# Attention and involution in one fp32 kernel: row sums by block transposes, another order of the first loads, and compute engines that keep the program's order

## The chip, the core and the metric

One core of a Trainium2 chip runs the whole program. Times are device microseconds of that core, in one launch. The engines are named as in the profile: PE is TensorE (PEld is its weight loads), DVE is VectorE, ACT is ScalarE, POOL is GpSimd, SP is SyncE, whose queue issues most of the DMAs.

## What is computed

The input `x` is 4 images of 512 channels and 64 x 64 pixels in fp32. Two layers follow each other. Cut to what matters:

```python
# layer 0: attention over the 4096 pixels of an image, 128 inner channels
q, k, v = wq @ x + bq, wk @ x + bk, wv @ x + bv        # each 128 x 4096
attn = softmax(q.T @ k, axis=-1)                       # 4096 x 4096
x = x + wo @ (v @ attn.T) + bo
# layer 1: involution, 7 x 7 taps whose weights are computed from the pixel
o = relu(s1 * (W1 @ x) + b1)                           # 128 channels
w = Ws @ relu(sr * (Wr @ o) + br) + bs                 # 49 taps x 8 groups, per pixel
x = x + s3 * (W3 @ sum_over_taps(w[tap, group] * shifted(o, tap))) + b3
```

## The kernel before

All that runs is `fast_path`. It computes the softmax without subtracting a maximum, and at its end it looks at every reciprocal of a row sum. If one lies outside of a safe range, the flag `verdict` sends the program into `general_path`, which repeats everything in the careful way. With these inputs the branch isn't taken.

**Keys and values.** For each image `b`, `keys_values` goes over 8 chunks of 512 pixels. A chunk costs four matmuls for `pk` and four for `pv` (512 input channels are 4 x 128), then `turn` transposes the values (`pvt`). Every fp32 matmul shows in the trace as two records.

**Attention.** Then `attention` goes over 8 blocks of 512 queries (the last two blocks of the last image are split into halves of 256) and for each block over 32 steps `j`. A step is one `score` matmul (`pss`, two steps ahead), an exponential on ACT (`pt`), one matmul of values by weights (`po`), and on DVE one addition `pacc<-pacc,pt` that sums the weights (lines 566 to 572).

**What is done between the steps.** After each step, and after every two matmuls of `keys_values`, `chores()` (line 223) takes one step of three generators. `finishing` holds `finish_block` of the block before: the row sums are added over the partitions by a matmul with a matrix of ones (`pl`, line 447), DVE takes the reciprocals in four pieces (`rl`, line 454), multiplies (`on`, line 457), then come `pwo` with an addition on DVE (line 463), `p1`, the transposes `pp` and the red layer `pr`; its `pause` calls and bare `yield`s are the numbers of steps between these. `closing` holds `turn_unit` and `close_chunk`: transposes `pa` of a finished sum, the matmuls `py` with W3 and an addition on DVE (line 367) for each. `pace()` takes taps of `involution`: each tap is a product on DVE (`prod`, line 291) and an addition on POOL (`acc`, line 315). A unit of the involution is 4 image rows; an image has 16 units.

**The planner.** `until`, `takes` and `free` keep an account of when PE, DVE and POOL will be free, with fixed costs (lines 64 to 68). It decides where in the program a tap is written: not while DVE has more than 3.5 us or POOL more than 7.5 us of work ahead of PE (line 269).

**The tail.** After the last step of the last image, `tail` is set (line 589), the waiting loops end at once, and a plain loop takes one step of `finishing`, one of `closing` and one tap in turn. In the tail every second tap is added not by POOL but by PE, as matmuls with the identity into `accp` (line 301):

```python
    while finishing or closing or units or more:
        step(finishing, 1)
        step(closing, 1)
        more = step(taps, 1)
```

**Buffers.** `pk` and `pss` share two PSUM buffers, `pl`, `pwo`, `p1`, `pp`, `pr`, `pq`, `pa` and `py` two others (tag `mm`); `pw` has one. The products have four buffers (`prods`), the exponentials five.

**The order on each engine.** The program gives a list of instructions. The library's scheduler may reorder them on each engine: it keeps the dependences and picks what its own model of the machine says is ready. What it picked is what the trace shows, and it isn't always the order in which the lines of the program are reached.

Of the kernel before, what the change touches and what calls it, by code (L numbers as in the profile page):

```python
# [8 lines left out]
F32 = mybir.dt.float32  # L9
AF = mybir.ActivationFunctionType  # L10
ALU = mybir.AluOpType
AX = mybir.AxisListType

B, C, H, W = 4, 512, 64, 64
N = H * W
P = 128
CT = C // P
CH = 512
NCH = N // CH
# [13 lines left out]
O_WK, O_WV, O_WQ, O_WO, O_W1, O_W3 = (i * 512 for i in range(6))  # L33
O_WP = 6 * 512
O_WT = O_WP + P
O_WR = O_WT + NTAP * G
# [7 lines left out]
V_BVC = V_BV + P  # L44
# [20 lines left out]
DVE_OP, POOL_OP = 0.7, 1.28  # L65
DVE_TAPS, POOL_TAPS = (0.16, 0.27), (0.19, 0.55)
ROW_US, X_US, PIX_US, LAND_US = 2.2, 3.8, 1.5, 3.0
HOP_US = 0.8

SAFE = (1e-30, 1e20)  # L70

# [2 lines left out]
def fast_path(  # L74
# [20 lines left out]
    nc = tc.nc  # L95

    def pool(name, bufs, **kw):
        return ctx.enter_context(tc.tile_pool(name=name, bufs=bufs, **kw))

    const = pool("const", 1)  # L100
    xpool = pool("x", 6)
# [3 lines left out]
    work1 = pool("work1", 1)  # L105
    work2 = pool("work2", 2)
    prods = pool("prods", 4)
    scratch = pool("scratch", 1, space=bass.MemoryType.DRAM)
    ps = pool("ps", 2, space=bass.MemoryType.PSUM)
    ps1 = pool("ps1", 1, space=bass.MemoryType.PSUM)  # L110

    wt = const.tile([P, O_WR], F32, name="wt")
    vec = const.tile([P, NVEC], F32, name="vec")
    ones = const.tile([P, P], F32, name="ones")
    ident = const.tile([P, P], F32, name="ident")
    rls = const.tile([B * NCH, CH], F32, name="rls")
    zero = const.tile([WP, PAD, P], F32, name="zero")
    ring = const.tile([P, RING, K, P], F32, name="ring")
    pix = [
# [3 lines left out]
    x_r = x.rearrange("b (t p) n -> b p t n", p=P)  # L123
# [16 lines left out]
    def until(us):  # L140
        while pe < us and not tail:
            yield "wait"

    def pe_us(us):
        nonlocal pe
        pe += us

    def takes(engine, us):
        free[engine] = max(free[engine], pe) + us
        return free[engine]  # L150

    def load_x(kind, b, c):
        xt = xpool.tile([P, CT, CH], F32, tag="x", name=f"{kind}_{b}_{c}")
        takes("dma", X_US)
        nc.sync.dma_start(xt, x_r[b, :, :, c * CH : (c + 1) * CH])
        return xt

    nc.sync.dma_start(wt[:, :O_WQ], wts[:, :O_WQ])
    nc.scalar.dma_start(vec, vecs)
    xa = {(0, c): load_x("xa", 0, c) for c in range(2)}  # L160
    xb = {}
    nc.scalar.dma_start(wt[:, O_WQ:], wts[:, O_WQ:O_WR])
    nc.gpsimd.memset(ones, 1.0)
    make_identity(nc, ident)
    nc.gpsimd.memset(zero, 0.0)

    def w_slice(off, t):
        return wt[:, off + t * P : off + (t + 1) * P]

    def v1(i):  # L170
        return vec[:, i : i + 1]

    def mm(o, lhsT, rhs, start=True, stop=True, shared=1):
        pe_us(rhs.free_size() * PE_COLUMN / shared)
        nc.tensor.matmul(o, lhsT=lhsT, rhs=rhs, start=start, stop=stop)  # L175

    def step(queue, n):
        while n and queue:
# [250 lines left out]
    def finish_block(b, c, off, n, po, sums):  # L429

        late = b == B - 1 and c >= NCH - 2
        name = f"{b}_{c}_{off}"
        xt = xb[b, c][:, :, off : off + n]

        def pause(us, steps):
            if late:
                yield from until(us + HOP_US)
            else:
                for _ in range(steps):
                    yield  # L440

        on = work2.tile([P, CH], F32, tag="on", name=f"on_{name}")[:, :n]
        nc.scalar.copy(on, po)
        yield from pause(free["dve"], 3)
        pl = ps.tile([P, CH], F32, tag="mm", name=f"pl_{name}")[:, :n]
        for i in range(CH // n):
            mm(pl, ones, sums[:, i * n : (i + 1) * n], i == 0, i == CH // n - 1)
        rl = work1.tile([P, CH], F32, tag="rl", name=f"rl_{name}")[:, :n]
        for i in range(n // P):
            if i == 0 or not late:  # L450
                yield
            cols = slice(i * P, (i + 1) * P)
            takes("dve", 0.9)
            nc.vector.reciprocal(rl[:, cols], pl[:, cols])  # L454
        row = b * NCH + c
        nc.sync.dma_start(rls[row : row + 1, off : off + n], rl[:1, :])
        nc.vector.tensor_tensor(on, on, rl, ALU.mult)
        yield from pause(takes("dve", DVE_OP * n / CH), 5)
        for t in range(CT):
            pw = ps.tile([P, CH], F32, tag="mm", name=f"pwo_{name}_{t}")[:, :n]  # L460
            mm(pw, w_slice(O_WO, t), on)
            takes("dve", DVE_OP * n / CH)
            nc.vector.scalar_tensor_tensor(  # L463
                xt[:, t, :], pw, bo[:, t : t + 1], xt[:, t, :], ALU.add, ALU.add
            )
            for _ in range(t % 2 if late else 1 + (t != 1)):
                yield
        p1 = ps.tile([P, CH], F32, tag="mm", name=f"p1_{name}")[:, :n]
        for t in range(CT):
            mm(p1, w_slice(O_W1, t), xt[:, t, :], t == 0, t == CT - 1)  # L470
            if t == 1 and not late:
                yield
        o1 = work1.tile([P, CH], F32, tag="o1", name=f"o1_{name}")[:, :n]
        nc.scalar.activation(o1, p1, AF.Relu, bias=v1(V_B1), scale=v1(V_S1))

        def last_bias():

            for t in range(CT):
                nc.scalar.activation(xt[:, t, :], xt[:, t, :], AF.Identity, bias=v1(V_B3 + t))  # L479
                if t % 2:  # L480
                    yield

        if late:
            yield from until(pe + HOP_US)
        else:
            yield from last_bias()

        tiles = n // P
        pp = ps.tile([P, CH // P, P], F32, tag="mm", name=f"pp_{name}")[:, :tiles]
        for t in range(tiles):  # L490
            nc.tensor.transpose(pp[:, t, :], o1[:, t * P : (t + 1) * P], ident)  # L491
        pe_us(0.5)
        o1t = work1.tile([P, CH // P, P], F32, tag="o1t", name=f"o1t_{name}")[:, :tiles]
        nc.scalar.copy(o1t, pp)
        top = c * RW + off // W
        for h in range(2):
            row = PAD + top + h
            nc.sync.dma_start(
                pix[b % 2][row : row + 2 * tiles - 1 : 2, PAD : PAD + W, :]
                .rearrange("r w c -> w r c"),  # L500
                o1t[h * W : (h + 1) * W],
            )
        us = takes("dma", PIX_US) + LAND_US
        pr = ps.tile([P, CH], F32, tag="mm", name=f"pr_{name}")[:, :n]
        mm(pr, w_slice(O_WP, 0), o1)
        red = redpool.tile([P, CH], F32, tag="red", name=f"red_{name}")[:, :n]
        nc.scalar.activation(red, pr, AF.Relu, bias=v1(V_BP), scale=v1(V_SP))
        for i in range(tiles // NT):
            reds[b, top // UR + i] = red, i * NT * P

        rows = top + n // W
        written[b] = rows, us
        units.extend((b, u) for u in range(top // UR, rows // UR))
        pump()
        yield
        if late:
            yield from last_bias()
# [61 lines left out]
    for b in range(B):  # L579
        kv = keys_values(b)  # L580
        if b == 0:

            pb = ps.tile([P, CT], F32, tag="mm", name="pb")
            for t in range(CT):
                mm(pb[:, t : t + 1], w_slice(O_WO, t), v1(V_BVC))
            bo = const.tile([P, CT], F32, name="bo")
            nc.vector.tensor_tensor(bo, pb, vec[:, V_BO : V_BO + CT], ALU.add)
        attention(b, *kv)
# [5 lines left out]
        more = step(taps, 1)  # L594


    ok = const.tile([B * NCH, CH], F32, name="ok")
    nc.vector.tensor_scalar(ok, rls, SAFE[0], None, ALU.is_ge)
    nc.vector.scalar_tensor_tensor(ok, rls, SAFE[1], ok, ALU.is_le, ALU.mult)
    okr = const.tile([B * NCH, 1], F32, name="okr")  # L600
    nc.vector.tensor_reduce(okr, ok, AX.X, ALU.min)
    pn = ps.tile([1, 1], F32, tag="mm", name="pn")
    nc.tensor.matmul(pn, lhsT=okr, rhs=ones[: B * NCH, :1], start=True, stop=True)
    nc.vector.tensor_scalar(verdict, pn, float(B * NCH) - 0.5, None, ALU.is_lt)


@with_exitstack
# [300 lines left out]


def attention_then_involution(tc, x, wts, vecs, out):  # L910
    nc = tc.nc
    with tc.tile_pool(name="verdict", bufs=1) as vpool:
        verdict = vpool.tile([1, 1], mybir.dt.int32, name="verdict")
        fast_path(tc, x, wts, vecs, out, verdict)
        again = nc.values_load(verdict[0:1, 0:1], min_val=0, max_val=1)
        with tc.If(again > 0):
            general_path(tc, x, wts, vecs, out)
# [85 lines left out]
```

## Time and profile before

| | |
|---|---|
| time, median of 3 runs | 2691.6 us (2691.48 to 2693.56) |
| span of the profiled run | 2689.5 us |
| PE busy | 2653.6 us, 99% |
| DVE busy | 1910.1 us, 71% |
| POOL busy | 1818.1 us, 68% |
| ACT busy | 894.4 us, 33% |
| DMA, mean rate over the span | 89 GB/s |
| first matmul of a key chunk starts at | 11.09 us |
| attention of the last block ends, DVE writes its last `sums` at | 2593.66 us |
| `verdict` written at | 2682.73 us |

In a group of the profile, the text names line, engine, operation, tile written `<-` tiles read and shapes; after the bar come the busy time in us and the mean ns of one, and after the second bar the idle time of that engine just before, with what ended it. In the timeline the columns are start, duration, engine, line, operation, tiles, and in brackets how long the engine sat idle before and for whom. Records of matmuls overlap in the timeline, so what one costs is read from the distance between starts: a 512-column fp32 matmul takes 0.86 us (two records).

### The profile page before, as it was taken

How to read it: one execution, taken by the hardware profiler on the slowest of the kernel's cores; microseconds unless marked ns; L12 is line 12 of the kernel's file. 1: busy time of each engine (PE TensorE's matmuls, PEld its weight loads, DVE VectorE, ACT ScalarE, POOL GpSimd, SP SyncE). 2: the span in 40 equal slices, each digit the busy share in tenths (PEclk: the TensorE clock that was granted, in tenths of full speed). 3: DMA queues.
4: the chain of work that ended last, by engine and by line, in shares of the span. 5: the costliest groups of instructions: out<-in, count | busy, mean ns of one | idle time of the engine just before them, and what ended most of it. 6: DMA issues, size and time to landing. Idle time of an engine off the chain costs nothing.

```text
span 2689.5 us, 23125 instructions
## 1 busy us (share of the span) xinstructions
PE 2653.6 (99%) x6932; PEld 1237.2 (46%) x6932; DVE 1910.1 (71%) x2635; ACT 894.4 (33%) x1495; POOL 1818.1 (68%) x1187
## 2 busy tenths in 40 slices
PE   8999999999999999999999999999999999999998
PEld 4444444444444444444444444444444444446874
DVE  0347888887475787888656678778847577888787
ACT  1333333332333333333233333333323333333420
POOL 0006788788681787878875478778877367887875
PEclk9999999999999999999999999999999999999999
DMA  7023223235614233323450423333453242332532
GB/s 239 21 56 68 68 74 78 59 90 137 182 39 104 59 90 90 91 70 77 131 148 23 104 59 90 90 91 90 106 148 103 44 99 67 79 71 59 116 79 83
DMA packets 109285, 240.07 MB, mean 89 GB/s; under 512 B 6296, under 2 KB 24928, under 8 KB 109024
## 3 DMA queue, kind: packets, MB, share of 16 engines
q1 hardware_dynamic: 108864, 237.10, 35.7%
q8 instruction: 56, 0.92, 0.1%
q10 hardware_dynamic: 288, 1.42, 0.1%
q14 instruction: 77, 0.63, 0.1%
HBM read 195.66 MB, written 42.77 MB: 89 GB/s over the span
## 4 chain that ended last, share of the span: by engine, by line
PE 96%; POOL 2%; DVE 1%; issue 0%; DMA 0%; ACT 0%; SPq 0%; POOLq 0%; ACTq 0%; DVEq 0%
PE pss L175 33%; PE po L175 33%; PE pq L175 4%; PE p L175 4%; PE pwo L175 4%; PE pv L175 4%; PE py L175 4%; PE pk L175 3%; PE pw L175 2%; POOL acc L315 2%; PE pl L175 1%; PE pr L175 1%; DVE prod L291 1%; PE accp L175 1%; PE pp L491 1%; PE pvt L383 1%
## 5 line engine op out<-in xcount | busy, mean ns | idle before, releaser
L315 POOL TENSOR_TENSOR acc<-acc,prod 128x768 f32<-128x768 f32 (+3 forms) x1059 | 1693.6, 1617 | 847.9 <-DVE prod L291 802.3
L175 PE MATMUL pss<-q,k 128*128 128x512 f32 (+1 forms) x2176 | 1051.1, 570 | 2.5 <-ACT q L425 2.5
L175 PE MATMUL po<-pt,v 128*128 128x512 f32 (+1 forms) x2176 | 1047.5, 568 | 0.0
L538 ACT ACTIVATE pt<-pss 128x512 f32<-128x512 f32 x1024 | 611.1, 597 | 1220.4 <-PE pss L175 1180.5
L291 DVE TENSOR_TENSOR prod<-ring,pw 128x512 f32<-128x512 f32 (+3 forms) x1092 | 894.2, 848 | 125.5 <-DMA ring<-pix 74.8
L569 DVE TENSOR_TENSOR pacc<-pacc,pt 128x512 f32<-128x512 f32 x956 | 662.1, 693 | 396.0 <-ACT pt L538 392.8
L175 PEld LDWEIGHTS po<-pt,v 128*128 128x128 f32 x2176 | 410.8, 190 | 469.7 <-issue 446.1
L175 PEld LDWEIGHTS pss<-q,k 128*128 128x128 f32 x2176 | 404.9, 190 | 460.8 <-issue 441.5
L175 PE MATMUL pwo<-on,wt 128*128 128x512 f32 (+1 forms) x272 | 132.7, 574 | 10.8 <-DVE xb L463 7.9
L367 DVE SCALAR_TENSOR_TENSOR xb<-py,vec,xb 128x512 f32<-128x512 f32 (+1 forms) x132 | 96.5, 731 | 58.2 <-PE py L175 55.7
L175 PE MATMUL py<-accT,wt 128*128 128x512 f32 (+1 forms) x264 | 131.1, 581 | 1.1 <-ACT accT L352 1.0
L454 DVE RECIPROCAL rl<-pl 128x128 f32<-128x128 f32 x128 | 120.2, 945 | 14.3 <-PE pl L175 14.3
L324 POOL TENSOR_TENSOR acc<-acc 128x512 f32<-128x512 f32 x120 | 123.4, 1028 | 9.4
L479 ACT ACTIVATE xb<-xb,vec 128x512 f32<-128x512 f32 (+1 forms) x136 | 93.8, 694 | 83.1 <-PE p L175 79.0
L175 PE MATMUL p<-xb,wt 128*128 128x512 f32 (+1 forms) x272 | 120.3, 567 | 0.0
L175 PE MATMUL pv<-xa,wt 128*128 128x512 f32 x256 | 118.9, 602 | 0.0
L175 PE MATMUL pk<-xa,wt 128*128 128x512 f32 x256 | 118.4, 600 | 0.3 <-DMA xa<-x_dram 0.3
L175 PE MATMUL pq<-xb,wt 128*128 128x512 f32 (+1 forms) x272 | 116.1, 567 | 0.0
L463 DVE SCALAR_TENSOR_TENSOR xb<-pwo,bo,xb 128x512 f32<-128x512 f32 (+1 forms) x136 | 96.9, 716 | 22.9 <-PE pwo L175 22.5
L291 DVE TENSOR_TENSOR acc<-ring,pw 128x1024 f32<-128x1024 f32 (+1 forms) x84 | 78.9, 958 | 29.0 <-PE pw L175 28.7
L567 DVE COPY pacc<-pt 128x512 f32<-128x512 f32 x34 | 23.5, 692 | 88.1 <-ACT pt L538 88.0
L175 PEld LDWEIGHTS pwo<-on,wt 128*128 128x128 f32 x272 | 51.9, 192 | 70.0 <-issue 48.6
(53 smaller groups left out, 891.5 us busy)
## 6 DMA issues: line engine op xcount, KB each, us to landing
ring<-pix SPq DMA_DIRECT2D x30, 1344.0 KB, 13.8
ring<-pix SPq DMA_DIRECT2D x38, 896.0 KB, 11.9
xa<-x_dram SPq DMA_DIRECT2D x32, 1024.0 KB, 5.9
xb<-x_dram SPq DMA_DIRECT2D x32, 1024.0 KB, 5.8
out_dram<-xb SPq DMA_DIRECT2D x31, 1024.0 KB, 4.2
ring<-pix SPq DMA_DIRECT2D x66, 448.0 KB, 9.9
ring<-pix SPq DMA_DIRECT2D x8, 2240.0 KB, 14.7
pix<-o1t SPq DMA_DIRECT2D x60, 128.0 KB, 2.5
```

The lines of the kernel that those rows point to most:

```text
L175: nc.tensor.matmul(o, lhsT=lhsT, rhs=rhs, start=start, stop=stop)
L291: nc.vector.tensor_tensor(prod[:, :, p0 : p0 + n, :].rearrange("p t d (g c) -> p t d g c", g=G), image.rearrange("p t d (g c) -> p t d g c ...
L315: nc.gpsimd.tensor_tensor(acc[:, :, d0 : d0 + n, :], acc[:, :, d0 : d0 + n, :], prod[:, :, :n, :], ALU.add,)
L324: nc.gpsimd.tensor_tensor(acc[:, :, :n, :], acc[:, :, :n, :], acc[:, :, n : 2 * n, :], ALU.add)
L367: nc.vector.scalar_tensor_tensor(xt[:, t, :], py, v1(V_S3 + t), xt[:, t, :], ALU.mult, ALU.add)
L383: nc.tensor.transpose(pvt[:, j, :], vs[:, j * P : (j + 1) * P], ident)
L454: nc.vector.reciprocal(rl[:, cols], pl[:, cols])
L463: nc.vector.scalar_tensor_tensor(xt[:, t, :], pw, bo[:, t : t + 1], xt[:, t, :], ALU.add, ALU.add)
L479: nc.scalar.activation(xt[:, t, :], xt[:, t, :], AF.Identity, bias=v1(V_B3 + t))
L491: nc.tensor.transpose(pp[:, t, :], o1[:, t * P : (t + 1) * P], ident)
L538: nc.scalar.activation(pt, pss, AF.Exp)
L569: nc.vector.tensor_tensor(paccs[k], paccs[k], pt, ALU.add)
```

## The change

It has three parts.

The **row sums** are added in another way. DVE adds the sums in groups of 32 columns with a transposed read (`blocks`, 128 x 16 instead of 128 x 512), a matmul with `quads` (four identities of 32 in each direction) of 16 columns adds over the partitions, one reciprocal takes 16 columns, a block transpose spreads them over 512 columns again (`spread`), and the multiplication follows. The reciprocals stay in SBUF, so a small DMA for each block (line 456) goes. The four steps between the reciprocals go too.

The **first loads** come in the order of their use: the weights of the keys, the first chunk of `x` in four pieces, the weights of the values, the second chunk, then the rest of the weights, all on one queue. The matmul `pb` for a bias is tied to its place in the program.

The **order**: `manual_schedule` makes PE, DVE, ACT and POOL take their instructions exactly as the program lists them. It is meant to let the planner's order stand as written.

```diff
-    nc.sync.dma_start(wt[:, :O_WQ], wts[:, :O_WQ])
+
     nc.scalar.dma_start(vec, vecs)
-    xa = {(0, c): load_x("xa", 0, c) for c in range(2)}
-    xb = {}
-    nc.scalar.dma_start(wt[:, O_WQ:], wts[:, O_WQ:O_WR])
+    nc.sync.dma_start(wt[:, :O_WV], wts[:, :O_WV])
+    xa, xb = {(0, 0): xpool.tile([P, CT, CH], F32, tag="x", name="xa_0_0")}, {}
+    for t in range(CT):
+        nc.sync.dma_start(xa[0, 0][:, t, :], x_r[0, :, t, :CH])
+    nc.sync.dma_start(wt[:, O_WV:O_WQ], wts[:, O_WV:O_WQ])
+    xa[0, 1] = load_x("xa", 0, 1)
+    nc.sync.dma_start(wt[:, O_WQ:], wts[:, O_WQ:O_WR])
...
+        blocks = work2.tile([P, CH // TB], F32, tag="blocks", name=f"blocks_{name}")
+        takes("dve", DVE_OP)
+        nc.vector.tensor_reduce(
+            blocks, sums.rearrange("p (k q) -> p k q", q=TB), AX.X, ALU.add, apply_transpose=True
+        )
         yield from pause(free["dve"], 3)
-        pl = ps.tile([P, CH], F32, tag="mm", name=f"pl_{name}")[:, :n]
+        pl = ps.tile([P, CH // TB], F32, tag="mm", name=f"pl_{name}")[:, : n // TB]
         for i in range(CH // n):
-            mm(pl, ones, sums[:, i * n : (i + 1) * n], i == 0, i == CH // n - 1)
-        rl = work1.tile([P, CH], F32, tag="rl", name=f"rl_{name}")[:, :n]
-        for i in range(n // P):
-            if i == 0 or not late:
-                yield
-            cols = slice(i * P, (i + 1) * P)
-            takes("dve", 0.9)
-            nc.vector.reciprocal(rl[:, cols], pl[:, cols])
-        row = b * NCH + c
-        nc.sync.dma_start(rls[row : row + 1, off : off + n], rl[:1, :])
-        nc.vector.tensor_tensor(on, on, rl, ALU.mult)
+            mm(pl, quads, blocks[:, i * n // TB : (i + 1) * n // TB], i == 0, i == CH // n - 1)
+        row = (b * N + c * CH + off) // TB
+        rl = rls[:, row : row + n // TB]
+        nc.vector.reciprocal(rl, pl)
+        spread = work1.tile([P, CH], F32, tag="rl", name=f"spread_{name}")[:, :n]
+        nc.vector.transpose(
+            spread.rearrange("p (k q) -> p k q", q=TB),
+            rl.unsqueeze(2).broadcast_to([P, n // TB, TB]),
+        )
+        nc.vector.tensor_tensor(on, on, spread, ALU.mult)
+        takes("dve", 0.3 + DVE_OP * n / CH)
         yield from pause(takes("dve", DVE_OP * n / CH), 5)
...
-                mm(pb[:, t : t + 1], w_slice(O_WO, t), v1(V_BVC))
+                tc.keep_in_program_order(mm(pb[:, t : t + 1], w_slice(O_WO, t), v1(V_BVC)))
...
-    ok = const.tile([B * NCH, CH], F32, name="ok")
+    ok = const.tile([P, B * N // TB], F32, name="ok")
...
-    nc.tensor.matmul(pn, lhsT=okr, rhs=ones[: B * NCH, :1], start=True, stop=True)
-    nc.vector.tensor_scalar(verdict, pn, float(B * NCH) - 0.5, None, ALU.is_lt)
+    nc.tensor.matmul(pn, lhsT=okr, rhs=ones[:, :1], start=True, stop=True)
+    nc.vector.tensor_scalar(verdict, pn, P - 0.5, None, ALU.is_lt)
...
-        fast_path(tc, x, wts, vecs, out, verdict)
+        with tc.manual_schedule(engines={E.PE, E.DVE, E.Activation, E.Pool}):
+            fast_path(tc, x, wts, vecs, out, verdict)
```

More of the change, by code (lines that the diff above doesn't have):

```diff
@@ L68 @@
 HOP_US = 0.8
+TB = 32
 SAFE = (1e-30, 1e20)
@@ L115, in fast_path @@
     ident = const.tile([P, P], F32, name="ident")
-    rls = const.tile([B * NCH, CH], F32, name="rls")
+    rls = const.tile([P, B * N // TB], F32, name="rls")
+    quads = const.tile([P, P], F32, name="quads")
     zero = const.tile([WP, PAD, P], F32, name="zero")
@@ L165, in fast_path @@
     nc.gpsimd.memset(zero, 0.0)
+    for i in range(P // TB):
+        corner = ident[:, i * TB : (i + 1) * TB]
+        if i == 0:
+            nc.gpsimd.tensor_copy(quads[:, :TB], corner)
+        else:
+            nc.gpsimd.tensor_tensor(quads[:, :TB], quads[:, :TB], corner, ALU.add)
+    for i in range(1, P // TB):
+        nc.gpsimd.tensor_copy(quads[:, i * TB : (i + 1) * TB], quads[:, :TB])
     def w_slice(off, t):
@@ L174, in mm @@
         pe_us(rhs.free_size() * PE_COLUMN / shared)
-        nc.tensor.matmul(o, lhsT=lhsT, rhs=rhs, start=start, stop=stop)
+        return nc.tensor.matmul(o, lhsT=lhsT, rhs=rhs, start=start, stop=stop)
     def step(queue, n):
@@ L594, in fast_path @@
         more = step(taps, 1)
-    ok = const.tile([B * NCH, CH], F32, name="ok")
+    ok = const.tile([P, B * N // TB], F32, name="ok")
     nc.vector.tensor_scalar(ok, rls, SAFE[0], None, ALU.is_ge)
     nc.vector.scalar_tensor_tensor(ok, rls, SAFE[1], ok, ALU.is_le, ALU.mult)
-    okr = const.tile([B * NCH, 1], F32, name="okr")
+    okr = const.tile([P, 1], F32, name="okr")
     nc.vector.tensor_reduce(okr, ok, AX.X, ALU.min)
     pn = ps.tile([1, 1], F32, tag="mm", name="pn")
-    nc.tensor.matmul(pn, lhsT=okr, rhs=ones[: B * NCH, :1], start=True, stop=True)
-    nc.vector.tensor_scalar(verdict, pn, float(B * NCH) - 0.5, None, ALU.is_lt)
+    nc.tensor.matmul(pn, lhsT=okr, rhs=ones[:, :1], start=True, stop=True)
+    nc.vector.tensor_scalar(verdict, pn, P - 0.5, None, ALU.is_lt)
 @with_exitstack
@@ L910, in attention_then_involution @@
 def attention_then_involution(tc, x, wts, vecs, out):
-    nc = tc.nc
+    nc, E = tc.nc, mybir.EngineType
     with tc.tile_pool(name="verdict", bufs=1) as vpool:
         verdict = vpool.tile([1, 1], mybir.dt.int32, name="verdict")
-        fast_path(tc, x, wts, vecs, out, verdict)
+        with tc.manual_schedule(engines={E.PE, E.DVE, E.Activation, E.Pool}):
+            fast_path(tc, x, wts, vecs, out, verdict)
         again = nc.values_load(verdict[0:1, 0:1], min_val=0, max_val=1)
```

## The prediction

> **What bounds the kernel now.** I read the page's parts 1, 2 and 4 first, then busy time by stage, then the timeline of PE and DVE where PE has gaps.
>
> ```profile
> PE 2653.6 (99%) x6932; PEld 1237.2 (46%) x6932; DVE 1910.1 (71%) x2635; ACT 894.4 (33%) x1495; POOL 1818.1 (68%) x1187
> PE 96%; POOL 2%; DVE 1%; issue 0%; DMA 0%; ACT 0%; SPq 0%; POOLq 0%; ACTq 0%; DVEq 0%
> ```
>
> PE is 99% busy and holds 96% of the chain that ended last: what leaves PE leaves the time, what makes PE wait is added. The stages (stretch, its length, then busy us of PE, PEld, DVE, ACT, POOL):
>
> ```profile
> 2080.00:2500.00 420.00, 419.99 (x1126) 203.77 (x1124) 315.56 (x439) 150.88 (x250) 289.94 (x188) 1.00 0.30 70
> 2594.00:2683.00 89.00, 79.32 (x286) 43.15 (x284) 73.00 (x98) 7.77 (x17) 59.73 (x38) 0.98 0.35 86
> ```
>
> Until the attention ends (2594 us) PE doesn't wait and DVE has a quarter of its time free. In the tail, 89 us, DVE works 73 and PE 79: both nearly full, and each feeds the other. The gaps, in order:
>
> ```profile
> 8.97 1.84 PE L175 MATMUL pb<-vec,wt 128*128 128x1 f32 x8 [8.97 <-DMA wt<-wts_dram]
> 11.09 5.19 PE L175 MATMUL pk<-xa,wt 128*128 128x512 f32 x8 [0.28 <-DMA xa<-x_dram]
> ...
> 1315.66 0.95 DVE L291 TENSOR_TENSOR prod<-ring,pw 128x768 f32<-128x768 f32 x1 [1.47 <-POOL acc L315]
> 1316.53 0.75 DVE L463 SCALAR_TENSOR_TENSOR xb<-pwo,bo,xb 128x512 f32<-128x512 f32 x1
> 1317.33 1.41 PE L175 MATMUL pwo<-on,wt 128*128 128x512 f32 x2 [2.62 <-DVE xb L463]
> ```
>
> PE starts at 11.09 us, `pb` (which the program lists after all keys) ahead of everything. At 1314 the addition of line 463, for a `pwo` that was done at about 1312, stands on DVE behind a tap that waits for POOL, and PE waits for its PSUM buffer. The same gap is at 664 and 1966.
>
> In the tail the order matters most:
>
> ```profile
> 2613.08 1.02 PE L175 MATMUL py<-accT,wt 128*128 128x512 f32 x2
> 2613.94 1.45 PE L175 MATMUL accp<-prod,ident 128*128 128x512 f32 x4
> 2615.23 1.88 PE L175 MATMUL py<-accT,wt 128*128 128x512 f32 x4
> ...
> 2614.81 1.81 DVE L291 TENSOR_TENSOR prod<-ring,pw 128x768 f32<-128x768 f32 x2
> 2616.54 0.74 DVE L367 SCALAR_TENSOR_TENSOR xb<-py,vec,xb 128x512 f32<-128x512 f32 x1
> 2617.20 0.94 DVE L291 TENSOR_TENSOR prod<-ring,pw 128x768 f32<-128x768 f32 x1
> ```
>
> Two `py` run back to back, which the program never lists, and DVE has taps to do while PE works: line 367 starts without an idle bracket.
>
> [...] here the first `pk` records are 0.98, 0.85, 0.85 us apart, then 0.43. Prices: [...] (the trace has 128-column transposes, each with its load, 0.11 us apart[...]; the trace has 690 for `sums`).
>
> **Part by part: what it gives.**
>
> Row sums. 30 matmuls `pl` of 512 columns (0.86 us from start to start) and 8 of 256 (0.43) are 29.2 us of PE. A 16-column matmul costs [...] 0.21 us (from below 0.05, if both loads hide, like the two records of `pn`, 0.026 apart; from above 0.43, the 0.214 between records of the one-column `pb`, which ran at the slow clock). 38 x 0.21 = 8.2, so **-21.0 us** (-13 to -27). On DVE four reciprocals of 945 ns (3.78) become a reduction and a transpose of 512 columns (0.69 each, by the price)[...]. That, the DMA of line 456 and a microsecond of POOL for `quads` count nothing: DVE waited 392.8 us for `pt` already, SP and POOL have gaps there. `pl` now waits for the reduction, 0.69 us later; in most blocks it came 6.98 us after `sums` started.
>
> First loads. Needed are 256 KB weights and 256 KB of `x`, with 99 KB of `vec` beside them. In the DMA view 226 KB are moved by 3.0 us, 443 by 3.75 and 792 by 4.5, so the 625 come by 4.2; a landing takes up to about 1 us more. First `pk` at 5.3 instead of 11.09: **-5.8** (-4.5 to -6.9). Later pieces arrive every 0.7 us, faster than cold matmuls use them. `pb` moves to after the keys: **+1.0**.
>
> Boundaries. In the program line 463 comes right after its `pwo`, ahead of later taps, and taps are listed only while the account has POOL at most 7.5 us behind. The three gaps (2.8 us each beyond a record) and the slow records after two of them (2.6) go: **-11** (-6 to -13).
>
> Shorter finish. The four steps between reciprocals (4 x 1.72 us) go, so image rows reach the involution earlier. Near the end taps are paced at 1.56 lines a us and POOL has only gaps of 3 to 5 us to give: the tail begins some 5 us of taps further on, **-3**.
>
> **What it costs.** On PE, DVE order in the middle hardly matters: the listed additions come earlier than now, and PE is already in program order there, but for three things.
>
> - At the end of the keys the transposes of the last chunk come before `pq`. Now one `pq` (0.86) fills the wait for ACT's copy (0.2 + 0.58); in program order PE waits. 4 x 0.87 = **+3.5**.
> - The first `pw` of each image is listed right behind `pr`, and needs ACT to have read `pr`. Now a `pss` runs first. In program order ACT still has two biases (0.69 each), an exponential (0.60), `o1t` (0.56) and the red layer (0.75) ahead: `pw` waits about 1.5. 4 times: **+6**.
> - `accp`, `pa`, `py` in the tail, below.
>
> The tail. There each round lists a step of `closing`, then a tap; a closing takes 9 rounds, so the taps in front of a `py` are fixed: an odd one, which PE adds. The listed sequence is tap (odd), its `accp`, `py`, line 367, tap (even), tap (odd), and so on. DVE now stands at line 367 until PE has done `accp` and `py`, and PE has nothing until DVE's next odd tap. With 0.86 us for each 512 columns, 0.1 and 0.2 for the two hand-overs: `accp` of three lines 1.29, of two 0.86, of four 1.72; `py` 0.86 (half size 0.43). DVE idles 2.45 us for each of three `py` of chunk 5 and 2.9 for the fourth, 2.0, 2.0, 2.0 and 2.45 for chunk 6, 2.0 and 2.0 for the first half of chunk 7: 22.2. Following both engines through the list by hand adds that the transposes `pa` of a unit (2.7 us on PE) now stand in front of `accp` and `py` (about 2.5 once), some buffer waits (2) and the last two `py` ahead of the last `pa` (0.9), and takes off 1.8 for the checks (below) that leave this stretch and about 2 for the faster sums: **+24** (18 to 30).
>
> The end. The checks of the reciprocals (lines 598 to 601: 0.40, 0.68, 0.67 us) ran at 2620 between taps; listed last, they stand between the last addition and `verdict`, on which the end hangs: with `pn` **+2.2**.
>
> Small waits elsewhere (an addition behind listed taps, `pl` for the reduction) +4, a PE that idles in the tail and slows its clock +3 (0 to 10): **+7**.
>
> Sum: -21.0 - 5.8 - 11 - 3 = -40.8; +1.0 + 3.5 + 6 + 24 + 2.2 + 7 = +43.7. That is +3: **2695 us**, no change that can be told, a little to the slow side.
>
> **The rivals.**
>
> - *Faster: the tail doesn't pay.* If the order of `accp` and `py` costs a third of the 24, because the tail begins further on and fewer `py` fall among odd taps, and the small waits stay near 0, the rest stands: 2695 - 16 - 7 = 2672. For it: PE and DVE both have idle time in the tail today (10 and 16 us). Against: the rounds fix which tap precedes a `py`.
> - *Slower: DVE becomes the wait everywhere.* In FIFO order a tap that waits for its rows (74.8 us in 17 waits now) or for POOL (50.5 us in 74) holds the additions behind it, and `pt`'s five buffers and the two of `mm` pass that on to PE. If a tenth of these 125 us arrives at PE and the clock stays low in the tail (+5 more): 2695 + 12 + 5 = 2712. For it: from 2500 to 2594 DVE is 82.3 of 94 us busy. Against: the long waits fall into the keys, where no `pacc` stands behind.
>
> **How the numbers follow.** The worked sum 0.44, the faster rival 0.31, the slower 0.25. The terms of the sum err by about 7 us together: within 5.4 us of 2691.6 about half of the first case, 0.23 with the edges of the others; slower 0.17 + 0.25 = 0.42; faster 0.05 + 0.30 = 0.35. The range takes in the middle of both rivals: 2668 to 2714.
>
> **What would show it.** First `pk` near 5.3 us. `pl` records of 16 columns with about 0.2 us a matmul, PE busy down by some 20 us ahead of 2594. No PE gap over 2 us at the image boundaries. DVE's last `sums` some 22 us earlier than 2593.7 (the gains without the shorter finish, 37.8, less 14.5 of waits and `pb`), near 2571. From there to `verdict` 112 to 118 us instead of 89, with line 367 waiting for `py` about 2 us a time and the checks after the last addition. I am wrong if the tail is as long as before (then 2672 or less), or if PE gets gaps in the attention (then over 2705).

## The result, and the profile after

| | before | after |
|---|---|---|
| time, median | 2692.31 us | 2752.43 us (2750.46 to 2757.48) |
| ratio | | 1.0224, 95% interval 1.0211 to 1.0237 |
| first `pk` starts | 11.09 us | 5.02 us |
| DVE starts its last `sums` | 2593.66 us | 2616.20 us |
| from there to `verdict` | 89.1 us | 126.9 us |

The change makes the kernel 60 us slower; 2695 was predicted, with a range up to 2714. In the profiles `verdict` comes 60 us later: 22.5 were lost before the last `sums`, where the forecast had some 22 gained, and 37.8 in the tail, where it had 23 to 29.

First the page's busy times and its chain of work that ended last:

```profile
PE 2650.3 (96%) x6932; PEld 1237.2 (45%) x6932; DVE 1860.3 (68%) x2609; ACT 879.2 (32%) x1495; POOL 1819.7 (66%) x1194
PE 90%; POOL 4%; DMA 3%; DVE 2%; issue 1%; ACT 0%; SPq 0%; POOLq 0%; ACTq 0%; DVEq 0%
```

PE's share fell from 99 to 96%, and a DMA, which held 0% of the chain before, now holds 3%. The stages (stretch, length, busy us of PE, PEld, DVE, ACT, POOL, then granted clock, DMA share, GB/s):

```profile
2080.00:2500.00 420.00, 419.13 (x1099) 197.75 (x1098) 304.34 (x429) 145.43 (x246) 281.10 (x182) 1.00 0.30 70
2616.00:2743.00 127.00, 90.73 (x278) 46.59 (x278) 75.05 (x99) 7.30 (x16) 59.84 (x38) 0.87 0.22 57
```

In the attention PE is as busy as before. In the tail DVE does 75 us of work (73 before) in 127 us instead of 89, and PE's clock is 0.87 instead of 0.98. The list of what PE waited for (total us, times, longest):

```profile
PE pk L191 <- DMA xa<-x_dram: 45.3, 4, 14.2
PE accp L191 <- DVE prod L307: 28.6, 14, 2.6
PE pw L191 <- ACT red L528: 3.5, 4, 0.9
...
PE pvt L399 <- ACT vs L431: 2.9, 4, 0.7
```

The 28.6 on `accp` is the tail and was forecast in kind; so were the last two lines. The first wasn't. Of its four waits one is the program's start (5.0 us); the other three are at the image boundaries. PE's timeline at the first of them:

```profile
690.64 3.60 PE L191 MATMUL pv<-xa,wt 128*128 128x512 f32 x8
707.13 5.54 PE L191 MATMUL pk<-xa,wt 128*128 128x512 f32 x8 [12.89 <-DMA xa<-x_dram]
```

The keys of the next image's last chunk wait 12.9 us for their `x`, and then eight records take 5.54 us instead of 3.60: the granted clock is 0.50 from 697.2 to 710.9 us. It is the same at 1353 and 2012 us, where the waits are 13.2 and 14.2 us and the eight records take 5.30 and 6.38, with the clock at 0.50 again. The gaps of 2.8 us behind line 463 are gone; something larger stands where they stood.

SP's timeline shows why `xa` is late. Before, then after:

```profile
690.04 1.28 SPq L498 DMA_DIRECT2D pix<-o1t  x2
691.41 0.56 SPq L155 DMA_DIRECT2D xa<-x_dram  x1
693.54 4.39 SPq L211 DMA_DIRECT2D ring<-pix  x6
```

```profile
677.31 6.89 SPq L227 DMA_DIRECT2D ring<-pix  x6
684.24 0.60 SPq L159 DMA_DIRECT2D xa<-x_dram  x1
```

Before, the load of the last key chunk stood ahead of the six `ring` loads that fetch the image's last rows for the involution; after, it stands behind them. The six are 2 x 448 and 4 x 896 KB, 4.5 MB. From 688 to 700 us the DMA engines move 215 GB/s, so the six take some 20 us (4.5 MB / 0.215), and this `xa`, whose like lands after a median 5.4 us, landed 22.8 us after its issue.

The finish of a block lists four steps less, so `pix` is written, and `pump()` lists the `ring` loads, earlier against the loop over the key chunks that lists `xa`. The prediction counted the four steps as a gain of 3 us and didn't follow them onto the queue.

### The profile page after: what moved, and what is told of

Read it like the earlier page. It is cut to its first block, busy times and chain, and to the rows that moved or that the text cites. A ratio compares the mean times of both kernels' runs of the same rounds, so it can differ in the third digit from the quotient of the medians.

```text
span 2748.7 us, 22972 instructions
## 1 busy us (share of the span) xinstructions
PE 2650.3 (96%) x6932; PEld 1237.2 (45%) x6932; DVE 1860.3 (68%) x2609; ACT 879.2 (32%) x1495; POOL 1819.7 (66%) x1194
## 4 chain that ended last, share of the span: by engine, by line
PE 90%; POOL 4%; DMA 3%; DVE 2%; issue 1%; ACT 0%; SPq 0%; POOLq 0%; ACTq 0%; DVEq 0%
PE pss L191 32%; PE po L191 32%; PE pq L191 4%; PE pwo L191 4%; POOL acc L331 4%; PE py L191 4%; PE p L191 4%; DMA xa<-x_dram 3%; PE pk L191 2%; PE pv L191 2%; PE pw L191 2%; PE accp L191 2%; DVE prod L307 1%; PE pr L191 1%; PE pa L357 0%
## 5 line engine op out<-in xcount | busy, mean ns | idle before, releaser
L191 PE MATMUL pk<-xa,wt 128*128 128x512 f32 x256 | 125.9, 634 | 45.3 <-DMA xa<-x_dram 45.3
L191 PEld LDWEIGHTS pk<-xa,wt 128*128 128x128 f32 x256 | 51.1, 204 | 109.9 <-issue 65.6
L500 ACT ACTIVATE xb<-xb,vec 128x512 f32<-128x512 f32 (+1 forms) x136 | 86.2, 686 | 0.0
L191 PE MATMUL accp<-prod,ident 128*128 128x512 f32 (+1 forms) x106 | 55.3, 662 | 28.7 <-DVE prod L307 28.6
## 6 DMA issues: line engine op xcount, KB each, us to landing
ring<-pix SPq DMA_DIRECT2D x8, 2240.0 KB, 24.6
```

The source lines that it names most:

```text
L191: return nc.tensor.matmul(o, lhsT=lhsT, rhs=rhs, start=start, stop=stop)
```

## The experiments

**Whose fault is the late load?** The queue theory: the missing four steps. The rival: the fixed order, by freeing an `x` buffer late. Four kernels, each against the kernel before.

The kernel after without the fixed order:

```diff
-        with tc.manual_schedule(engines={E.PE, E.DVE, E.Activation, E.Pool}):
-            fast_path(tc, x, wts, vecs, out, verdict)
+        fast_path(tc, x, wts, vecs, out, verdict)
```

> The change without the fixed order: row sums and first loads as in the kernel after, the scheduler orders the engines. Queue theory (the last key chunk's x load stands behind six ring loads, because a block's finish is four steps shorter): PE still waits about 13 us for xa at each of three image boundaries, the tail is back near 89 us; 2752 less 38 (tail) less 8 (transposes of the values, first pw) = about 2706. Order theory (the fixed order frees the x buffers late and so delays the load): no wait for xa, row sums -21, loads -6, finish -3: about 2663.

Measured: 2715.5 us, ratio 1.0080 (1.0063 to 1.0097). The load of the last key chunk still comes behind the six `ring` loads and lands 24.6 us after its issue. PE doesn't wait in the form that was expected: the scheduler lets it run `pq` first, and then it waits on taps (7.7 us for `prod`, 3.8 for POOL) until 715.9 us, where `pk` of the last chunk starts. The order theory's 2663 is out: the load is late without the fixed order too.

The kernel before with the fixed order alone:

```diff
-        fast_path(tc, x, wts, vecs, out, verdict)
+        with tc.manual_schedule(engines={E.PE, E.DVE, E.Activation, E.Pool}):
+            fast_path(tc, x, wts, vecs, out, verdict)
```

> The kernel before with the fixed order alone. Queue theory: no wait for xa (the finish has its four steps, so xa is issued ahead of the ring loads); boundary gaps of 2.8 us gone (-11), transposes of the values +3.5, first pw +4, tail 89 -> 127 (+38): about 2727. Order theory: the same and PE waits about 13 us for xa three times: about 2768.

Measured: 2737.1 us, 1.0161 (1.0144 to 1.0178). PE waits for `xa` once, at the start. The last `sums` starts at 2592.6, 1.0 us earlier than before, and the tail takes 138.0 us. So with the old sums the order alone gives nothing up to the tail and costs 49 us in it; the expectation, with the tail of the kernel after, was 10 us short.

The kernel after with the four steps put back between `pl` and the reciprocal:

```diff
+        for i in range(n // P):
+            if i == 0 or not late:
+                yield
         row = (b * N + c * CH + off) // TB
```

> The kernel after, with the four steps put back between pl and the reciprocal. Queue theory: xa is issued ahead of the ring loads again, the three waits of PE for xa (40.8 us) and some 5 us of slow matmuls after them go, about 3 us come back for the later finish: about 2709. Order theory: the waits stay, about 2752.

Measured: 2704.0 us, 1.0043 (1.0028 to 1.0057): 48 us off the kernel after. SP's timeline is again in the order of before, and in PE's the `pk` of the last chunk follows its `pv` (689.77 + 3.43):

```profile
681.35 0.60 SPq L159 DMA_DIRECT2D xa<-x_dram  x1
683.60 4.18 SPq L227 DMA_DIRECT2D ring<-pix  x6
```

```profile
689.77 3.60 PE L191 MATMUL pv<-xa,wt 128*128 128x512 f32 x8
693.20 3.60 PE L191 MATMUL pk<-xa,wt 128*128 128x512 f32 x8
```

`xa` was issued only 2.9 us earlier than in the kernel after and landed in 9.1 us instead of 22.8.

The four steps move more than the queue. So the last kernel of the four keeps the short finish and holds back the `ring` loads alone:

```diff
-        while load // STEP in written:
+        while load // STEP in written and not held:
...
+            if c == NCH - 2 and held:
+                held.pop()
+                pump()
...
+            if b and c == 4:
+                held.append(True)
```

> The kernel after, the finish as short as there, but the ring loads of the last rows of an image are held back in the program until the load of the last key chunk stands ahead of them. Queue theory: the three waits for xa go, 2752 - 46 = about 2706. Bandwidth rival (the DMA engines are full at the boundary, whichever load comes first): PE still waits over 8 us each time, over 2737.

Measured: 2705.2 us, 1.0044 (1.0027 to 1.0061), with `xa` landing in 9.2 us and no wait for it at the boundaries. (The same 4480 KB of `ring` rows now go in four loads instead of six.) Two different edits that share only the place of this load give the same time. That settles 47 to 48 of the 60 us. It also shows no gain of the shorter finish with the queue mended (2705.2 against 2704.0).

The late load is that dear only together with the fixed order. Without the order, the four steps make 14 us (2715.5 above, against 2701.5 for the same kernel with the four steps, further below): the scheduler gives PE other work while the load is late. In the fixed order PE stands in front of `pk` until it lands, and the same steps make 48.

**Is it one queue's order, or the DMA engines' load?** In the kernel after, only this load is moved to ACT's queue:

```diff
-                xa[b, c + 1] = load_x("xa", b, c + 1)
+                xa[b, c + 1] = load_x("xa", b, c + 1, nc.scalar if b and c + 1 == NCH - 1 else nc.sync)
```

> The kernel after, with only the load of the last key chunk of images 2 to 4 issued from ACT's queue; the six ring loads stay where they are on SP's. If xa is late because it stands behind the ring loads in one queue, it lands some 10 us after its issue and the three waits go or fall below 3 us: about 2712. If all queues share what is already handed to the DMA engines, so that xa waits for the ring data whichever queue it comes from, the waits stay near 13 us: about 2750. If ACT must wait for the x buffer, PE waits for its exponentials or biases instead.

Measured: 2746.6 us, 1.0196 (1.0179 to 1.0213). ACT reaches the issue at 687.11, 2.9 us later than SP did, and `xa` lands 18.7 us after it; PE waits 11.9 us at this boundary:

```profile
706.12 5.55 PE L191 MATMUL pk<-xa,wt 128*128 128x512 f32 x8 [11.90 <-DMA xa<-x_dram]
```

A queue of its own helps little, 5.8 us (2752.4 to 2746.6). In the DMA view of 670 to 712 us the packets of SP's queue take 89.5% of the time of the 16 DMA engines, and those of ACT's 10.5%. From 687.2 to 693.4 us, right after the issue, it shows 375 packets of SP's queue and none of ACT's; from 693.5 to 705.2 us it shows 528 packets of ACT's queue beside 543 of SP's, 90 and 156 GB/s. What the load waited for in the first 6 us isn't shown. What helps is to issue it ahead of the `ring` loads (2704.0 and 2705.2 us, above).

**What makes the tail long?** The theory: DVE stands at the addition of line 383 until PE has added the tap before it and computed `py`, and PE then has nothing. The kernel after shows it in the timeline:

```profile
2645.42 0.75 DVE L383 SCALAR_TENSOR_TENSOR xb<-py,vec,xb 128x512 f32<-128x512 f32 x1 [1.65 <-PE py L191]
2646.09 1.81 DVE L307 TENSOR_TENSOR prod<-ring,pw 128x768 f32<-128x768 f32 x2
2647.09 1.56 PE L191 MATMUL accp<-prod,ident 128*128 128x512 f32 x4 [1.70 <-DVE prod L307]
2648.48 1.02 PE L191 MATMUL py<-accT,wt 128*128 128x512 f32 x2
2649.54 0.75 DVE L383 SCALAR_TENSOR_TENSOR xb<-py,vec,xb 128x512 f32<-128x512 f32 x1 [1.64 <-PE py L191]
```

One round is 4.12 us (2645.42 to 2649.54). DVE has 2.5 us of work in it and PE 2.2: neither is the bound, the alternation is. With the four steps back, the addition is listed one tap after its `py`, the number of steps unchanged:

```diff
             takes("dve", DVE_OP * n / CH)
+            if tail:
+                yield
             nc.vector.scalar_tensor_tensor(
                 xt[:, t, :], py, v1(V_S3 + t), xt[:, t, :], ALU.mult, ALU.add
             )
-            for _ in range(2):
+            for _ in range(1 if tail else 2):
                 yield
```

> The kernel with the four steps back (2704), and in the tail DVE's addition of a py is listed one round, that is one tap, after its matmul. If the tail is long because DVE stands at the addition until PE has done accp and py, about ten waits of 1.9 to 2.5 us on DVE and the gaps of PE before accp shrink to under 1 us: 15 to 20 us less, about 2686. If the tail is long because PE runs slow there or has more taps left, it stays within 5 us of 2704.

Measured: 2690.3 us, 0.9990 (0.9984 to 0.9997): 14 us off, a little less than expected. The tail takes 114.1 us, and the round is now 2.6 us (2595.52 to 2598.11), with no wait in front of the addition. Between `py` and `accp`, where PE lost 23.1 us in the kernel after, it still loses 12.4:

```profile
2595.52 0.74 DVE L385 SCALAR_TENSOR_TENSOR xb<-py,vec,xb 128x512 f32<-128x512 f32 x1
2595.66 1.56 PE L191 MATMUL accp<-prod,ident 128*128 128x512 f32 x4 [0.42 <-DVE prod L307]
2596.18 1.81 DVE L307 TENSOR_TENSOR prod<-ring,pw 128x768 f32<-128x768 f32 x2
2597.05 1.02 PE L191 MATMUL py<-accT,wt 128*128 128x512 f32 x2
2598.05 1.56 PE L191 MATMUL accp<-prod,ident 128*128 128x512 f32 x4
2598.11 0.75 DVE L385 SCALAR_TENSOR_TENSOR xb<-py,vec,xb 128x512 f32<-128x512 f32 x1
```

Then, with the addition back in its place and the four steps kept, the fixed order ends where the tail begins, and the scheduler orders the rest:

```diff
+    order = ExitStack()
+    order.enter_context(tc.manual_schedule(engines={E.PE, E.DVE, E.Activation, E.Pool}))
...
+    order.close()
     tail.append(True)
...
-        with tc.manual_schedule(engines={E.PE, E.DVE, E.Activation, E.Pool}):
-            fast_path(tc, x, wts, vecs, out, verdict)
+        fast_path(tc, x, wts, vecs, out, verdict)
```

> The kernel with the four steps back (2704), the fixed order ending where the tail begins, so that the scheduler orders the tail. If the order makes the tail long, it falls from 127.6 to about 90 us: 2667. If what is left to do at its beginning makes it long, it stays above 115: over 2692.

Measured: 2664.6 us, 0.9896 (0.9881 to 0.9911). The tail is 86.3 us, at clock 0.98:

```profile
2570.00:2656.00 86.00, 77.36 (x278) 41.44 (x278) 73.44 (x98) 7.71 (x17) 60.23 (x38) 0.98 0.32 81
```

The work is the same as in the 127 us above; the order alone makes it long. This version is 28 us faster than before.

**The two other parts, alone.** The row sums in the kernel before (old loads, the four steps kept, the scheduler's order; their diff is the one of the change):

> The kernel before with the row sums alone (first loads as before, the four steps kept, the scheduler's order). The forecast's step gives -21: about 2672. If a pl of 16 columns holds PE for 0.43 us as its upper bound had it, -13: about 2680.

Measured: 2706.2 us, 1.0050 (1.0034 to 1.0065). Neither expectation holds: they cost 13 us. Yet on PE they do what was forecast: the matmuls `pl`, each from its start to the next start, take 5.9 us in all instead of 29.5. The loss is at the boundaries, where PE now waits up to 8.5 us for the addition after `pwo` (29.4 us in 7 waits; before, 7.9 in 3). To see whether the order mends it, the row sums, the first loads and the four steps were run without any fixed order:

> Row sums, first loads and the four steps back, all engines in the scheduler's order: the row sums alone gave 2706.2 and the loads alone -4.9, so 2701, with PE waiting 8 us three times for additions (line 487) that stand behind waiting taps. Against 2664.6 with the order up to the tail: the order would be worth some 36 us in the middle. If it were worth only the 11 of the forecast, 2676.

Measured: 2701.5 us, 1.0031 (1.0019 to 1.0042), as expected. Its DVE and PE at the first boundary:

```profile
658.28 0.95 DVE L307 TENSOR_TENSOR prod<-ring,pw 128x768 f32<-128x768 f32 x1 [1.48 <-POOL acc L331]
660.70 0.95 DVE L307 TENSOR_TENSOR prod<-ring,pw 128x768 f32<-128x768 f32 x1 [1.47 <-POOL acc L331]
663.12 0.95 DVE L307 TENSOR_TENSOR prod<-ring,pw 128x768 f32<-128x768 f32 x1 [1.47 <-POOL acc L331]
665.01 0.95 DVE L307 TENSOR_TENSOR prod<-ring,pw 128x768 f32<-128x768 f32 x1 [0.93 <-POOL acc L331]
665.88 0.74 DVE L487 SCALAR_TENSOR_TENSOR xb<-pwo,bo,xb 128x512 f32<-128x512 f32 x1
666.68 2.08 PE L191 MATMUL pwo<-on,wt 128*128 128x512 f32 x2 [8.48 <-DVE xb L487]
```

The addition stands behind taps that each wait for POOL, as at 1314 us in the kernel before, with more taps. Against 2664.6 the order up to the tail is worth 37 us here. In the profiles the last `sums` starts 29.5 us later than there, and the tail takes 4.6 us more (90.9 against 86.3). Why the scheduler puts more taps ahead with the new sums was not looked into.

The first loads in the kernel before, alone (with `pb` tied to its place):

> The kernel before with the first loads alone (and pb tied to its place). The forecast's step gives -5.8 and +1.0: about 2688. If the earlier start is half lost because PE runs its first seven matmuls at half speed instead of three, 2690.

Measured: 2688.3 us, 0.9984 (0.9978 to 0.9991), that is -4.9 (-5.9 to -2.4). In the profiles the first `pk` starts 6.1 us earlier, the first `pss` of the attention only 3.0 (72.7 against 75.7): seven of the first records are slow (0.85 us to the next instead of 0.43) instead of three, which costs 1.7; `pb` takes 0.8, and PE waits 0.7 for a `pvt`.

**Can the two small costs be had back?** In the version of 2664.6 us, first the last transposes `pvt` are listed behind `pq`, then also the first `pw` of an image a step later:

```diff
-        turn(NCH - 1, last)
-        return kt, vT
+        return kt, vT, lambda: turn(NCH - 1, last)
...
         qs[0] = queries(b, *blocks[0])
+        last_turn()
```

> The best so far (2664.6: four steps back, order up to the tail), with the transposes of the last values listed after pq instead of before it. The forecast's step (+3.5 for their wait, traced at 4 x 0.9 us): about 2661. If another wait takes its place (pss for q), 2664 to 2665.

```diff
+            if units[0][1] == 0 and not tail:
+                yield "wait"
             b, u = units.pop(0)
```

> As the kernel with the later transposes, and the first pw of an image listed a step after pr. Its wait of 1.03 us, four times, less what the taps lose by starting later: about 2657 to 2658. If the step only moves the wait, 2661.

Measured: 2658.1 us (0.9870, 0.9855 to 0.9886) and 2655.2 us (0.9858, 0.9842 to 0.9875). The first gave 6.5 us, more than its four waits of 0.9. In the profiles an image gains 1.4 us, since `q`, now computed first, keeps `pss` waiting less too (1.6 us in all against 3.4), and some 1.4 us come from the start, where four of the first records are slow instead of seven, which the edit doesn't touch. The second gave 2.9. The last version beats both kernels, by 38 us (2693.4 in the same rounds) and by 97.

## Why the prediction was wrong

The step that failed is **shorter finish, -3**. It looked at taps only and set down a gain, where the edit cost 47 to 48 us: it put 4.5 MB of `ring` loads ahead of the last `xa`, and in the fixed order that gave PE three waits of 12.9 to 14.2 us (40.3) and some 6 us of slow matmuls behind them (1.9 at the first, from 5.54 - 3.60). So the sign "No PE gap over 2 us at the image boundaries" failed too, although the mechanism of **boundaries, -11** held: the gaps behind line 463 went. With the load back in its place, the last `sums` starts at 2568.5 us; 2571 had been forecast for it. The sum for everything up to the tail was near but for a transfer that it left out. "PE gets gaps in the attention (then over 2705)" was named as what would make it wrong; the gaps came from the keys and a DMA, not from DVE as in the slower rival.

The second miss is a size, **tail, +24** with the clock's +3 and +2.2 for the checks: 112 to 118 us were forecast, 126.9 came. The main term was right: PE loses 23.1 us between `py` and `accp` (0.6 before), where the sum had 22.2 of idle DVE (its ten terms make 22.7, which changes nothing). Too small was what stands around it. The last finishes inside the tail, in fixed order, lose about 5 us on PE (`pl` to `pwo` 2.3, `pwo` to `accp` 1.8 more than before, `p1` to `pp` 0.8), for which nothing was set down. Neighbouring records of `accp`, of `py` and of `pwo`, between which PE waits for nothing, lose 7.2 more than in the tail before (5.3 of it on `accp`), not 3; the granted clock is 0.87 against 0.98. The checks ahead of `pn` cost 2.3, beside 2.2. Two waits of `accp` behind `pw`, 5.6, stand where PE lost 4.6 behind `pw` before.

The rest, by its steps:

- **Row sums, -21.** `pl` fell from 29.5 to 5.9 us, 0.16 us a matmul where 0.21 was forecast, an estimate of the author's (two of the transposes `pvt` in the trace before, each with its load, take 2 x 0.109 us from start to start): right for PE. On DVE, by shape (busy us, mean ns):

```profile
L462 DVE TRANSPOSE_TENSOR_REDUCE blocks<-sums 128x16 f32<-128x512 f32 x34 | 24.2, 711 | 1.2
L473 DVE STREAM_TRANSPOSE spread<-rls 128x512 f32<-128x512 f32 x30 | 21.3, 712 | 1.0
L471 DVE RECIPROCAL rls<-pl 128x16 f32<-128x16 f32 x30 | 7.7, 256 | 61.6 <-PE pl L191 61.6
```

  711 and 712 ns where 690 was taken, the mean of `sums` before; the reciprocal of 16 columns takes 256. But alone, in the scheduler's order, the row sums cost 13. In the program's order no run has them by themselves. Of the run with the order alone and the one with the four steps back, the second starts its last `sums` 24.1 us earlier and its first `pss` 5.8 (71.7 against 77.5), which are the loads. From these figures an estimate is 18 us for the row sums up to the tail. The two parts depend on each other, and the prediction added them up.
- **First loads, -5.8 and +1.0.** -4.9 alone, so right within the noise; the 3.0 that the profiles show are less, for the slow first records, which the sum had at nothing.
- **Last transposes, +3.5.** PE loses 897 ns in front of them four times, 3.6 us: right.
- **First `pw`, +6.** 1.03 us four times: two thirds of it.
- **The faster rival** (the tail doesn't pay, 2672) was wrong on the tail. The scheduler's tail with the queue mended gives 2664.6, near it for another reason.

## What to carry to other kernels

When an edit takes steps out of a program whose DMAs are listed between steps, write down the order of the DMA queue before and after: here a load of 1 MB behind 4.5 MB of slow ones cost 48 us, more than all the gains of the forecast (40.8), and issuing it 3 us earlier, ahead of them, was enough to have it back. In this kernel the fixed order was worth most where additions otherwise stood behind taps that waited (37 us with the new row sums), and cost most where two nearly full engines feed each other in turn (a tail of 127.6 us instead of 86.3); it can be held for one stretch and let go for the next. Two parts of a change may each look bad alone and good together (row sums +13, order +43, the two with the first loads, the queue mended and the tail left free -28), so their worth couldn't be summed from one baseline.

## What wasn't expected of the hardware

- The `ring` loads move at about 215 GB/s with the DMA engines eight to nine tenths busy; when they were done, from 704 to 708 us, `x` loads moved at 386 GB/s. The same megabytes are not the same time.
- PE's granted clock falls in the tail at a gap of little over 2 us, and not at every one. In the kernel after, `py` to `accp` at 2654.09 us takes 2.65 us from start to start, 2.2 of them without a matmul. The granted clock is 0.50 from 2656.47 to 2659.88 us, and the records of `accp` there come 1.01, 0.85, 0.85 and 0.64 us apart instead of 0.43. Three gaps of 2.30 before it, at 2640.7 to 2648.9, have no such records behind them (0.53, then 0.43 apart). The trace shows a pattern. In this run the stretches at 0.50 begin only at whole multiples of 3.413 us from each other (2618.92, 2656.47, 2676.95 us are 11 and 6 apart). In the step of that raster before 2656.47, PE is busy for 1.62 of 3.41 us, 47%; in the four steps before it, 1.85 to 2.42 us, 54 to 71%. In this run every step at full clock in which PE was busy 47% or less was followed by half the clock, and none of 53% or more was. This is what one run shows, not a rule. A chain of short gaps is to be costed with a slower clock too: 0.87 granted over the whole tail.
- The load that was issued from ACT's queue behind the backlog of SP's moved nothing for 6.3 to 6.4 us, at all three boundaries (from 687.1, 1345.1 and 2003.2 us), and then moved 528 packets beside 543 of SP's (at the first, up to 705.2 us).
